# Gated attention outputs transposed on VectorE, with blocks exchanged through DRAM, in one transformer layer on Trainium2

## The chip, the cores and the metric

The kernel runs on one core of one Trainium2 chip. The metric is the device time of one execution in microseconds (us), as the median of several runs. A core has five engines that work side by side, each with its own queue of instructions: TensorE (PE in the profile; its weight loads are listed apart as PEld), VectorE (DVE), ScalarE (ACT), GpSimd (POOL) and SyncE (SP), which here only issues transfers. They read and write the on-chip memory SBUF; TensorE writes its results into PSUM, which is used as eight banks of 128 x 512 fp32. Transfers between SBUF and DRAM are done by 16 DMA engines.

## The reference

The layer takes x of shape 8 x 256 x 256 (2048 tokens of width 256), normalises it, and adds to it an attention part and a feed-forward part. Cut to what matters here:

```python
xn = layernorm(x)
q, k = rope(xn @ Wq.T), rope(xn @ Wk.T)          # 16 heads of 128
v, g = xn @ Wv.T, xn @ Wg.T
s = clip(xn @ Ws1.T @ Ws2.T + bs2, -32, 32)      # 16 heads of 64 states
z = cumlogsumexp(s, axis=time); es, enz = exp(s), exp(-z)
A  = tril(q @ k.T * scale)
qv = softmax(enz * (A @ es))
W2 = tril((qv * enz) @ es.T)
o  = W2 @ v                                      # per head: tokens x 128
o_g = o * rsqrt(mean(o * o) + EPS) * g_norm_weight * (g * sigmoid(g))
attn = o_g.reshape(B, T, 16 * 128) @ Wo.T
ffn  = (gelu(xn @ Wgate.T) * (xn @ Wup.T)) @ Wdown.T   # weights are 4-bit codes with scales
out  = x + attn + ffn
```

The change concerns the step between `o_g` and the product with `Wo`. The product contracts over the 128 values of a head, so `o_g`, which comes out with tokens on the partitions, has to be turned until the values of a head lie on the partitions.

## The kernel before, in words

All data is fp32. The 2048 tokens are worked on in four groups of 512 (`G`), and the 16 heads in eight pairs. One step of the main loop is one group and one pair: 32 steps (`N`), and the loop runs over `n` from -1 to 32, because the work of a pair is spread over three turns of the loop. In turn `n` the kernel makes the queries and keys (`rope`) of step `n + 1`, the values, gates, scores, logits and softmax of step `n`, and the turning of the softmax, the weights, the outputs and the closing product of step `n - 1` or `n - 2`. Between them stand pieces of the feed-forward part (`ffn`), which are spread over the whole run by a planned number for each turn.

The order is written out by hand. `POS` gives each piece a place between 0 and 1 within its turn (`START` overrides it in the first turns, `NORM_AT` places the norm of the next group), the list of pieces is sorted by that place, and the pieces are called in that order. A piece issues its TensorE work at once and hands what follows on the other engines to a generator (`chain`). After each piece `tick` moves every open chain on by one stage; `need` ticks until the named chains are done. `new` takes a buffer of a tag and first lets the users of its previous tenant finish. So the order in which each engine's instructions stand is settled when the program is built; on the chip the engines wait for one another through semaphores.

The pieces around the change are these.

- `outputs` (L656), once for each head of a pair, multiplies the weights with the values into the PSUM bank `po`, four blocks of 128 tokens by 128 values (L665). Its chain squares them on ScalarE (L674, with a sum for each token), adds on VectorE (L678), takes the power -1/2 on GpSimd (L679), and writes the gated output `og` with four VectorE instructions, one for each block (L683). `og` is laid out token block by token block, each of 128 contiguous values.
- `turn_back` (L690), once for each head, transposes the four blocks of `og` on TensorE into a bank (L696), and ScalarE copies that bank to `ogT` (L700). In `ogT` the 128 tokens of a block are contiguous in each partition.
- `close` (L705) runs in every second turn, for two pairs together, in two halves of 256 tokens. Each half is eight matmuls (L714): two token blocks times four heads, with a block of `ogT` as the weights and 256 columns of `w_o` moving. The result is added to `res` on VectorE (L277, by `add_to`), and a finished part of `res` goes out to DRAM (L270).

An fp32 matmul is two passes on TensorE, each with its own weight load, so that the 256 matmuls of `close` stand in the profile as 512; a transpose is one pass.

SyncE's queue carries all other transfers: the weights of a step (`load_w`, L161, two transfers a step), the packed feed-forward weights (L227 and L228), the rows of x (L152), and the output. A transfer at its head that waits for a buffer holds up those behind it.

Other lines that the prediction names: L205 transposes the normalised rows, whose columns it takes two apart; L298 and L318 are the feed-forward gate and up products; L338 the down product; L444 the queries and keys; L455 their first rotation product on VectorE; L496 values and gates; L514, L517 and L504 the scores and their mask; L562 the maximum of the softmax; L255 the last stage of decoding a feed-forward weight; L632 and L633 the masked weights `wt`.

Of the kernel before, what the change touches and what calls it, by code (L numbers as in the profile page):

```python
# [10 lines left out]
F32 = mybir.dt.float32  # L11
# [6 lines left out]
P = 128  # L18
# [4 lines left out]
G = 512  # L23
NG = NTOK // G
TC = G // P
# [6 lines left out]

POS = {'scores': (0.059, 0.112),
 'turn': (0,),
 'logits': (0.144,),
 'softmax': (0.232,),
 'cross': (0.179,),
 'weights': (0.179, 0.193),
 'low': (0.072,),
 'states': (0.223,),  # L40
 'outputs': (0.364, 0.394),
 'back': (0.647, 0.688),
 'close': (0.136, 0.286),
 'rope': (0.36, 0.45, 0.487, 0.63),
 'vg': (0.458, 0.566, 0.766, 0.838)}
START = {-1: {'states': (0.544,), 'rope': (0.14, 0.43, 0.53, 0.63)},
# [5 lines left out]
     'rope': (0.198, 0.24, 0.32, 0.45)}}  # L52
FEED = {-1: (0.452, 1.0)}
NORMS = {0: 1, 2: 2, 5: 3}
NORM_AT = (0.2, 0.293, 0.427, 0.58, 0.75, 0.938)
FIRST = [0.35, 1.41]
LAST = [2.16, 2.05]
DUE = [4, 6, 7, 7, 8, 8, 9, 10, 11, 12, 12, 13, 14, 15, 15, 16, 17, 18, 19, 19, 19, 22, 23, 23, 24]
# [3 lines left out]
def layer_kernel(ctx: ExitStack, tc: tile.TileContext, a: dict, out: bass.AP):  # L62
# [19 lines left out]
    ln = ctx.enter_context(tc.tile_pool(name="ln", bufs=1))  # L82
    ff = ctx.enter_context(tc.tile_pool(name="ff", bufs=2))
    de = ctx.enter_context(tc.tile_pool(name="de", bufs=1))
    aw = ctx.enter_context(tc.tile_pool(name="aw", bufs=1))
    p1 = ctx.enter_context(tc.tile_pool(name="p1", bufs=1))
    p2 = ctx.enter_context(tc.tile_pool(name="p2", bufs=2))
# [5 lines left out]
    def need(*gens):  # L93

        while any(c in chains for c in gens):
            tick()
# [7 lines left out]
    def new(pool, shape, tag, bufs=1, dtype=F32):  # L104

        users = held.setdefault(tag, [])
        if len(users) >= bufs:
            need(*users[-bufs])
        t = pool.tile(shape, dtype, tag=tag, name=tag, bufs=bufs)
        users.append([])  # L110
        at_tag[id(t)] = t, users[-1]
        return t
# [3 lines left out]
    def chain(gen, *tiles):  # L116

        chains.append(gen)
        for t in tiles:
            at_tag[id(t)][1].append(gen)  # L120
        return gen

    def bank():
        return new(ps_p, [P, 512], "ps", 8)
# [233 lines left out]
    sin_b = sin.unsqueeze(1).to_broadcast([P, 2, T])  # L358
    of = {n: {} for n in range(N)}
    rTs = {}  # L360

    def load_wo():
        nc.sync.dma_start(out=gw, in_=a["gw"])
# [292 lines left out]
    def outputs(n, j):  # L656

        to = of[n]
        wt, c = to["wt", j]
        need(c, *(to["sg", i] for i in (0, 2)))  # L660
        v, sg, eps = to["v"], to["sg"], to["eps"]
        pot = to["po"][j]
        po = pot.rearrange("p (i d) -> p i d", d=DK)
        for i in range(TC):
            nc.tensor.matmul(  # L665
                po[:, i, :], lhsT=wt[:, i, :], rhs=v[:, i, j * DK : (j + 1) * DK],
                start=False, stop=i == TC - 1,
            )
        ss = new(p2, [P, TC], "ss", 2)
        og = new(p2, [P, TC, DK], "og", 2)  # L670

        def work():
            for i in range(TC):
                nc.scalar.activation(  # L674
                    og[:, i, :], po[:, i, :], AF.Square, accum_out=ss[:, i : i + 1]
                )
            yield
            nc.vector.scalar_tensor_tensor(ss, ss, 1.0 / DK, eps[:, j::2], ALU.mult, ALU.add)  # L678
            nc.gpsimd.tensor_tensor(ss, ss, nhalf, ALU.pow)  # L679
            yield  # L680
            yield
            for i in range(TC):
                nc.vector.scalar_tensor_tensor(  # L683
                    og[:, i, :], po[:, i, :], ss[:, i : i + 1],
                    sg[:, i, j * DK : (j + 1) * DK], ALU.mult, ALU.mult,
                )

        to["og", j] = og, chain(work(), pot, ss, og, eps, sg)

    def turn_back(n, j):  # L690

        og, c = of[n]["og", j]
        need(c)
        ps = bank()
        for i in range(TC):
            nc.tensor.transpose(ps[:, i * P : (i + 1) * P], og[:, i, :], ident)  # L696
        ogT = new(p2, [P, G], "ogT", 4)

        def work():
            nc.scalar.copy(ogT, ps)  # L700
            yield

        of[n]["ogT", j] = ogT, chain(work(), ps, ogT)

    def close(n, i):  # L705

        g, hp = steps[n]
        ogT = [of[m]["ogT", j] for m in (n - 1, n) for j in range(2)]
        need(*(c for _, c in ogT))
        pst = bank()  # L710
        ps = pst.rearrange("p (i d) -> p i d", i=2)
        for k in range(2):
            for hh in range(4):
                nc.tensor.matmul(  # L714
                    ps[:, k, :], lhsT=ogT[hh][0][:, (i + k) * P : (i + k + 1) * P],
                    rhs=w_o[:, (hp // 2) * 4 + hh, :], start=hh == 0, stop=hh == 3,
                )
        chain(add_to(g * TC + i, ps), pst)
# [11 lines left out]
    for n in range(-1, N + 1):  # L730
# [43 lines left out]
        if n > 0:  # L774
            put("turn", 0, turn, n - 1)
            put("cross", 0, cross, n - 1)
            put("weights", 0, weights, n - 1)
            put("weights", 1, apply, n - 1)
            for k in range(2):
                put("outputs", k, outputs, n - 1, k)  # L780
                put("back", k, turn_back, n - 1, k)
            if n % 2 == 1 and n > 1:
                for k in range(2):
                    put("close", k, close, n - 2, 2 * k)
            if n == N:
                for k in range(2):
                    put_at(2.0, close, N - 1, 2 * k)
# [80 lines left out]
```

## Time and profile before

The three runs took 1257.07, 1257.10 and 1257.87 us, median 1257.1. The profile is of one further execution:

| | |
|---|---|
| profiled execution, as timed | 1258.18 us |
| its span, first to last instruction | 1256.2 us |
| mean granted TensorE clock | 0.997 |
| DMA, all 16 engines | 47.96 MB in 18431 packets, mean 38 GB/s |
| weights load `wts`, 64 of 512 KB | 3.7 us from issue to landing (median) |
| output store `out_dram`, 8 of 256 KB | 2.2 us from issue to landing (median) |

The span lies inside the timed execution; the 2 us between them are outside the instructions. "Busy" is the time in which an engine has at least one instruction in work. Matmuls overlap in the pipeline, so the mean length of one is longer than the distance between the starts of two. Where the profile names a wait, it names the instruction whose end came last before the start. L numbers are lines of the kernel before unless the text says otherwise.

### The profile page before, as it was taken

The page shows a single profiled execution, that of the slowest core. Times are in us where ns is not written, and L with a number is a line of the kernel's source. Part 1 is how long each engine was busy: PE and PEld are TensorE (multiplying, and loading weights), DVE is VectorE, ACT ScalarE, POOL GpSimd, SP SyncE. Part 2 cuts the span into 40 slices and gives each one's busy share as a digit, 9 for nine tenths or more (in the row PEclk, how much of TensorE's full clock was granted, in tenths as well). Part 3 has the DMA queues.
Part 4 walks back from the last instruction along what each step waited for, and adds up shares of the span by engine and source line. Part 5 has one row for each costly group of instructions (what it writes and reads, how often), then busy time and mean ns, then how long its engine had stood idle before and what let it go on. Part 6 is the DMA issues. An engine that isn't in the chain of part 4 may idle for free.

```text
span 1256.2 us, 18066 instructions
## 1 busy us (share of the span) xinstructions
PE 1236.6 (98%) x6704; PEld 889.1 (71%) x6704; DVE 798.8 (64%) x1592; ACT 541.9 (43%) x1709; POOL 441.3 (35%) x408
## 2 busy tenths in 40 slices
PE   6999999999999999999999999999999999999998
PEld 3576776777776777767677676776777766777776
DVE  4977655767665676564776656666655566566443
ACT  3344435444344544443543534445443355444232
POOL 3524334432244443233442423444232444322311
PEclk9999999999999999999999999999999999999999
DMA  5211111011111100111110111110011110101100
GB/s 158 84 49 51 51 34 51 19 33 34 51 35 34 51 18 18 34 35 51 50 35 1 34 34 51 34 34 25 10 34 34 35 34 28 41 17 34 34 17 17
DMA packets 18431, 47.96 MB, mean 38 GB/s; under 512 B 2020, under 2 KB 6500, under 8 KB 18344
## 3 DMA queue, kind: packets, MB, share of 16 engines
q1 hardware_dynamic: 17912, 46.55, 11.8%
q8 instruction: 53, 0.87, 0.3%
q10 hardware_dynamic: 432, 0.26, 0.1%
q14 instruction: 34, 0.28, 0.1%
HBM read 44.71 MB, written 2.10 MB: 37 GB/s over the span
## 4 chain that ended last, share of the span: by engine, by line
PE 92%; DVE 5%; DMA 1%; issue 1%; POOL 1%; ACT 0%; POOLq 0%; ACTq 0%; SPq 0%; DVEq 0%
PE ps L496 16%; PE ps L444 16%; PE ps L714 9%; PE ps L338 9%; PE ps L298 8%; PE ps L318 8%; PE ps L514 4%; PE ps L665 4%; PE ps L533 4%; PE ps L624 3%; PE ps L517 2%; PE ps L696 2%; PE ps L406 2%; PE ps L554 1%; DMA pk<-in_codes_dram 1%; PE ps L601 1%
## 5 line engine op out<-in xcount | busy, mean ns | idle before, releaser
L457 POOL TENSOR_TENSOR z<-z,sin 128x512 f32<-128x512 f32 x128 | 163.3, 1276 | 416.8 <-ACT z L454 416.2
L444 PE MATMUL ps<-xT,wts 128*128 128x512 f32 x512 | 243.5, 599 | 0.7 <-ACT xT L211 0.7
L496 PE MATMUL ps<-wts,xT 128*128 128x256 f32 x1024 | 236.6, 379 | 0.0
L496 PEld LDWEIGHTS ps<-wts,xT 128*128 128x128 f32 x1024 | 193.2, 190 | 57.4 <-issue 26.8
L444 PEld LDWEIGHTS ps<-xT,wts 128*128 128x128 f32 x512 | 95.2, 193 | 80.4 <-issue 72.6
L306 POOL TENSOR_SCALAR t<-t 128x512 f32<-128x512 f32 x64 | 40.4, 631 | 261.7 <-ACT t L304 259.6
L453 ACT COPY z<-ps 64x512 f32<-64x512 f32 x128 | 74.5, 582 | 129.7 <-PE ps L444 90.5
L298 PE MATMUL ps<-xT,w_gate 128*128 128x512 f32 x256 | 121.5, 597 | 4.3 <-DVE t L312 2.2
L318 PE MATMUL ps<-xT,w_up 128*128 128x512 f32 x256 | 120.5, 593 | 0.0
L433 DVE RECIPROCAL enz<-enz 128x128 f32<-128x128 f32 x128 | 117.0, 932 | 0.0
L338 PE MATMUL ps<-w_down,inter 128*128 128x256 f32 x512 | 115.9, 379 | 0.2 <-DVE inter L326 0.2
L714 PE MATMUL ps<-w_o,ogT 128*128 128x256 f32 x512 | 115.6, 379 | 0.0
L277 DVE TENSOR_TENSOR res<-ps,res 128x512 f32<-128x512 f32 x64 | 44.1, 689 | 112.3 <-PE ps L338 57.5
L714 PEld LDWEIGHTS ps<-w_o,ogT 128*128 128x128 f32 x512 | 95.7, 190 | 15.1 <-issue 2.6
L338 PEld LDWEIGHTS ps<-w_down,inter 128*128 128x128 f32 x512 | 96.0, 190 | 13.3 <-DVE inter L326 0.6
L458 POOL TENSOR_TENSOR q<-q,z 128x512 f32<-128x512 f32 x64 | 81.5, 1273 | 27.9 <-DVE q L455 23.8
L458 POOL TENSOR_TENSOR k<-k,z 128x512 f32<-128x512 f32 x64 | 81.3, 1270 | 19.3 <-DVE k L455 15.4
L455 DVE TENSOR_TENSOR k<-ps,cos 128x512 f32<-128x512 f32 x64 | 43.8, 684 | 63.2 <-ACT z L454 63.2
L683 DVE SCALAR_TENSOR_TENSOR og<-ps,ss,sgate 128x128 f32<-128x128 f32 x256 | 71.0, 341 | 19.4 <-POOL ss L679 18.6
L310 ACT ACTIVATE t<-t 128x512 f32<-128x512 f32 x64 | 40.3, 630 | 97.8 <-DVE t L308 97.8
L609 ACT COPY cross<-ps 128x256 f32<-128x256 f32 x32 | 11.9, 372 | 161.3 <-PE ps L601 160.8
L566 ACT ACTIVATE pr<-ps,mx 128x64 f32<-128x64 f32 x256 | 76.3, 323 | 12.1 <-DVE mx L563 12.1
(81 smaller groups left out, 2002.8 us busy)
## 6 DMA issues: line engine op xcount, KB each, us to landing
wts<-in_wqkvg_dram SPq DMA_DIRECT2D x64, 512.0 KB, 3.7
pk<-in_codes_dram SPq DMA_DIRECT2D x12, 256.0 KB, 4.6
sc<-in_scales_dram SPq DMA_DIRECT2D x12, 256.0 KB, 4.7
w_o<-in_wo_dram SPq DMA_DIRECT2D x4, 512.0 KB, 7.0
out_dram<-res SPq DMA_DIRECT2D x8, 256.0 KB, 2.2
res<-in_x_dram SPq DMA_DIRECT2D x3, 512.0 KB
res<-in_x_dram SPq DMA_DIRECT2D x2, 256.0 KB, 4.3
w_s<-in_ws_dram SPq DMA_DIRECT2D x4, 68.0 KB
```

The costliest lines, as they stand in the source:

```text
L298: nc.tensor.matmul(pg, lhsT=w_gate[:, c, ns], rhs=xT[:, c, gs], start=c == 0, stop=c == 1)
L318: nc.tensor.matmul(pu, lhsT=w_up[:, c, ns], rhs=xT[:, c, gs], start=c == 0, stop=c == 1)
L338: nc.tensor.matmul(ps[:, k, :], lhsT=inter[g, n][0][:, (i + k) * P : (i + k + 1) * P], rhs=w_dn[:, n, :], start=n == 2 * q, stop=n == 2 * ...
L433: nc.vector.reciprocal(r, r)
L444: nc.tensor.matmul(ps, lhsT=w[:, c, :], rhs=xT[:, c, g * G : (g + 1) * G], start=c == 0, stop=c == 1)
L453: nc.scalar.copy(z[0:64], pv[64:128])
L457: nc.gpsimd.tensor_tensor(z, z, sin_b, ALU.mult)
L458: nc.gpsimd.tensor_tensor(y, y, z, ALU.add)
L496: nc.tensor.matmul(ps[:, k, :], lhsT=xT[:, c, tt], rhs=w[:, which, c, :], start=c == 0, stop=c == 1,)
L566: nc.scalar.activation(pr[:, k, :], pv[:, k, :], AF.Exp, bias=mx[:, k : k + 1], scale=SCALE, accum_out=sm[:, k : k + 1],)
L683: nc.vector.scalar_tensor_tensor(og[:, i, :], po[:, i, :], ss[:, i : i + 1], sg[:, i, j * DK : (j + 1) * DK], ALU.mult, ALU.mult,)
L714: nc.tensor.matmul(ps[:, k, :], lhsT=ogT[hh][0][:, (i + k) * P : (i + k + 1) * P], rhs=w_o[:, (hp // 2) * 4 + hh, :], start=hh == 0, stop= ...
```

## The change

`turn_back` and its place in the order are gone. `outputs` now writes `og` with the four token blocks innermost: value by value, the four blocks side by side, so that each of the four gate instructions writes with a step of four elements (16 bytes). The squares, whose values nobody reads, still go to the same buffer in contiguous pieces. A second chain then waits for the first, transposes `og` in place on VectorE in blocks of 32 x 32 (`turn_blocks`, one instruction of 128 x 512 for each head), and exchanges the blocks: each band of 32 partitions is stored to a DRAM scratch `by_way` (four transfers of 64 KB in pieces of 512 bytes), and one transfer of 256 KB brings the scratch back as `ogT` (`exchange`). `ogT` too has the token blocks innermost, so that `close` reads its weights with a step of four elements. Some places in the order change as well.

```diff
 POS = {'scores': (0.059, 0.112),
  'turn': (0,),
- 'logits': (0.144,),
+ 'logits': (0.178,),
...
- 'low': (0.072,),
+ 'low': (0,),
...
- 'back': (0.647, 0.688),
- 'close': (0.136, 0.286),
+ 'close': (0.107, 0.365),
...
-NORM_AT = (0.2, 0.293, 0.427, 0.58, 0.75, 0.938)
+NORM_AT = (0.29, 0.293, 0.427, 0.58, 0.75, 0.938)
...
+    dram = ctx.enter_context(tc.tile_pool(name="dram", bufs=1, space=bass.MemoryType.DRAM))
...
+    def turn_blocks(t):
+        v = t.rearrange("p (c k) i -> p c i k", c=4)
+        nc.vector.transpose(v, v)
+
+    def exchange(to, t):
+        by_way = dram.tile([P, 4, 32 * TC], F32, tag="by_way", name="by_way", bufs=4)
+        for r in range(4):
+            nc.sync.dma_start(
+                out=by_way.rearrange("(c k) r x -> r k c x", c=4)[r],
+                in_=t[32 * r : 32 * (r + 1)].rearrange("p (c k) i -> p c (k i)", c=4),
+            )
+        yield
+        nc.sync.dma_start(
+            out=to.rearrange("p t i -> p (t i)"), in_=by_way.rearrange("p r x -> p (r x)")
+        )
...
         ss = new(p2, [P, TC], "ss", 2)
-        og = new(p2, [P, TC, DK], "og", 2)
+        og = new(p2, [P, DK, TC], "og", 2)
+        ogT = new(p2, [P, P, TC], "ogT", 4)
+        flat = og.rearrange("p d i -> p (d i)")
 
         def work():
             for i in range(TC):
                 nc.scalar.activation(
-                    og[:, i, :], po[:, i, :], AF.Square, accum_out=ss[:, i : i + 1]
+                    flat[:, i * DK : (i + 1) * DK], po[:, i, :], AF.Square,
+                    accum_out=ss[:, i : i + 1],
                 )
...
                 nc.vector.scalar_tensor_tensor(
-                    og[:, i, :], po[:, i, :], ss[:, i : i + 1],
+                    og[:, :, i], po[:, i, :], ss[:, i : i + 1],
                     sg[:, i, j * DK : (j + 1) * DK], ALU.mult, ALU.mult,
                 )
 
-        to["og", j] = og, chain(work(), pot, ss, og, eps, sg)
-
-    def turn_back(n, j):
-
-        og, c = of[n]["og", j]
-        need(c)
-        ps = bank()
-        for i in range(TC):
-            nc.tensor.transpose(ps[:, i * P : (i + 1) * P], og[:, i, :], ident)
-        ogT = new(p2, [P, G], "ogT", 4)
-
-        def work():
-            nc.scalar.copy(ogT, ps)
-            yield
-
-        of[n]["ogT", j] = ogT, chain(work(), ps, ogT)
+        def turned():
+            while first in chains:
+                yield
+            turn_blocks(og)
+            yield
+            yield from exchange(ogT, og)
+
+        first = chain(work(), pot, ss, og, eps, sg)
+        to["ogT", j] = ogT, chain(turned(), og, ogT)
...
                 nc.tensor.matmul(
-                    ps[:, k, :], lhsT=ogT[hh][0][:, (i + k) * P : (i + k + 1) * P],
+                    ps[:, k, :], lhsT=ogT[hh][0][:, :, i + k],
                     rhs=w_o[:, (hp // 2) * 4 + hh, :], start=hh == 0, stop=hh == 3,
                 )
...
             for k in range(2):
                 put("outputs", k, outputs, n - 1, k)
-                put("back", k, turn_back, n - 1, k)
```

## The prediction

> **What bounds the kernel now.** I read the page's busy shares first, then its slices, then the chain that ended last. Columns of the first line: busy us, share of the span, instructions.
>
> ```profile
> PE 1236.6 (98%) x6704; PEld 889.1 (71%) x6704; DVE 798.8 (64%) x1592; ACT 541.9 (43%) x1709; POOL 441.3 (35%) x408
> ...
> PE   6999999999999999999999999999999999999998
> ...
> PE 92%; DVE 5%; DMA 1%; issue 1%; POOL 1%; ACT 0%; POOLq 0%; ACTq 0%; SPq 0%; DVEq 0%
> ```
>
> TensorE is full in every slice but the first and the last, at a granted clock of 0.997, and 92% of the chain is its own work. So I asked for TensorE's waits alone (total us, times, longest):
>
> ```profile
> PE ps L205 <- DVE z L197: 7.9, 2, 7.3
> PE ps L298 <- DVE t L312: 2.2, 1, 2.2
> ```
>
> The whole list is eight rows and 16 us. Asked for 75 to 1235 us alone, it holds only the second row, one stall at 134 us; in 180 to 1235 TensorE is busy 1055.00 of 1055 us. A microsecond of its work removed there is a microsecond of the kernel, unless something else becomes late. Next come the groups by shape that the change touches (xcount | busy us, mean ns | idle before):
>
> ```profile
> L714 PEld LDWEIGHTS ps<-w_o,ogT 128*128 128x128 f32 x512 | 95.7, 190 | 15.1 <-issue 2.6 <-DVE at L504 0.5 <-ACT t L310 0.2
> ...
> L683 DVE SCALAR_TENSOR_TENSOR og<-ps,ss,sgate 128x128 f32<-128x128 f32 x256 | 71.0, 341 | 19.4 <-POOL ss L679 18.6
> ...
> L700 ACT COPY ogT<-ps 128x512 f32<-128x512 f32 x64 | 34.3, 585 | 1.5 <-PE ps L696 1.0
> L696 PE MATMUL ps<-ident,og 128*128 128x128 f32 x256 | 33.6, 273 | 0.0
> ```
>
> A matmul's 273 ns is its length through the pipe, not what it costs its successor. The cost is the distance of starts, from TensorE's timeline (start us, length us):
>
> ```profile
> 540.77 1.04 PE L696 MATMUL ps<-ident,og 128*128 128x128 f32 x8
> 541.64 1.88 PE L298 MATMUL ps<-xT,w_gate 128*128 128x512 f32 x4
> ```
>
> Eight transposes take 541.64 - 540.77 = 0.87 us, 0.109 us each. In the same way the 16 closing matmuls at L714 (521.78 to 525.23) are 0.216 us apart, and L665's 16 (528.66 to 530.45) 0.112.
>
> **What the Trainium skill says.** "TensorE: Matmul & The Clock Gate", Step-by-step: the next weights are loaded while the present matmul runs. The trace agrees: each load starts with the matmul before it. So a load costs nothing until it is longer than that matmul's 0.216 us. "SBUF — State Buffer", Door 1: the memory has 16-byte lines, and at least two hits in a line are needed for full rate. The changed close reads its weights four fp32 apart, one hit in a line. The only strided weights in this trace are the layer norm's, two fp32 apart, two hits in a line:
>
> ```profile
> 252.90 0.65 PEld L205 LDWEIGHTS ps<-ident,z 128*128 128x128 f32 x4
> 253.11 0.63 PE L205 MATMUL ps<-ident,z 128*128 128x128 f32 x4
> ...
> 253.58 0.60 PE L583 MATMUL ps<-ident,pr 128*128 128x128 f32 x4
> ```
>
> These four are 0.118 us apart ((253.58 - 253.11)/4) against 0.109, and their loads are 204 ns long against 141 ns for L696: here two hits are not quite free. "VectorE: DVE Perf Modes", The three transpose paths: VectorE transposes only within 32x32 blocks, and 311 ns for 128x128 bf16. No VectorE transpose stands in this trace.
>
> **The change part by part**, against the profiled execution: span 1256.2 us, 1258.2 us as timed, 1.1 us above the median of 1257.1.
>
> 1. Removed from TensorE: 32 steps x 2 heads x 4 transposes = 256 x 0.109 = 27.9 us. All stand after 94 us, where TensorE is full. The chain gives the same rows 2.1% of the span, 26.4 us. I take -27.9.
>
> 2. Removed from ScalarE: 64 copies x 0.585 = 37.4 us, and 64 uses of a PSUM bank. ScalarE is busy 43% and off the path: 0, a little slack for others.
>
> 3. Added to VectorE: 64 transposes of 128x512. Nearest rows by shape: the reduction L562 over 128x512 at 678 ns, and from above L255 into w_up, 1238 ns for 128x512. I take 0.68 us each, 43.5 us in all, and keep 0.6 to 1.24. The gate's four writes now go 16 bytes apart: 341 ns each if the step is free, some 474 if it doubles the 133 ns that 128 cycles at 0.96 GHz take (the page's clock, an estimate). VectorE rises from 799 to 843 us, at worst 912 of some 1230: 69 to 74%. In a step this is 1.4 us, at worst 3.5. Behind it in the queue stand k, q and res, then idle time:
>
> ```profile
> 571.01 1.13 DVE L683 SCALAR_TENSOR_TENSOR og<-ps,ss,sgate 128x128 f32<-128x128 f32 x4 [1.12 <-POOL ss L679]
> 572.05 0.68 DVE L455 TENSOR_TENSOR k<-ps,cos 128x512 f32<-128x512 f32 x1
> 572.65 0.68 DVE L455 TENSOR_TENSOR q<-ps,cos 128x512 f32<-128x512 f32 x1
> 574.29 0.69 DVE L277 TENSOR_TENSOR res<-ps,res 128x512 f32<-128x512 f32 x1 [0.96 <-PE ps L338]
> 577.28 0.69 DVE L455 TENSOR_TENSOR k<-ps,cos 128x512 f32<-128x512 f32 x1 [2.31 <-ACT z L454]
> ```
>
> The brackets hold 1.12, 0.96 and 2.31 us: the first transpose falls into the first, the second is made good by 577. Those waiting are PSUM banks and the scores, which TensorE reaches ten us later. I take 1.5 us over the whole run (0.05 a step); bounds 0 and 10 (0.3 a step).
>
> 4. The close's weights: 512 loads, now four apart. If the price goes by the element, as at step two, they stand 0.118 us apart and hide under 0.216: 0. At twice the unit spacing, 0.224, they cost 8 ns x 512 = 4 us; at 0.24, 12 us. I take 0 because step two cost only 9 ns more spacing; the upper end is a rival below.
>
> 5. Added transfers: per head four stores of 64 KB and one load of 256 KB, 64 x 5 = 320 issues, 33.6 MB. The DMA engines are about 12% busy. Rows for landing, from the page's list of issues: the 256 KB output store 2.2 us, the 512 KB weight load 3.7. SyncE's timeline at the start shows 0.33 to 0.46 us for most issues, so one exchange is 4 x 0.4 + 2.2 + 0.4 + 3.7 = 7.9 us, of which the issuing queue is held for 4.2. The order of the changed program shows, on SyncE, stores, load, stores, load, then the two weight loads of the step, so these go out up to some 8 us later; they are wanted after more than 20 us. The rows themselves are wanted at the next even step's close, some 17 us after 572 (the close at 590.24, about 1 us earlier now), against 0.7 + 7.9 plus the other head's 4.2 = 12.8. Hidden.
>
> 6. At the end that cover is thin. The last gate ends at 1235.9, and the close that needs it starts at 1245.20, its fourth matmul 1.3 us later; less the transposes gone from between (1.1 us), the rows are wanted at 1245.4. The first head's gate ends at 1232.9, its transpose at 1233.6, its load goes out at 1237.6. Then the second head's stores: +1.6 +2.2 +0.4 +3.7 = 1245.5. I take 0.5 us; bounds 0 and 2.5.
>
> 7. Moved: on TensorE each pair's second close stands after the first head's output matmuls, not before; the low-rank product, the logits and one norm shift by a few places. Nothing is issued twice; beside steps without a close, which run without waits today, the new order looks alike. 0; bounds -1 and +2.
>
> Sum: -27.9 + 1.5 + 0.5 + 0.5 (half of point 7's upper margin) = -25.4; 1258.2 - 25.4 = 1232.8 as profiled, 1231.7 beside the median. **Forecast 1232 us.**
>
> **The rivals.**
> A: the strided weights show partly, at 0.224 to 0.25 us: 512 x 8 to 34 ns, +4 to +17 us, 1236 to 1249. For it: one hit in a line is worse than two. Against: the step to two cost 9 ns.
> B: VectorE or the exchange becomes late in each step, because TensorE's step shrinks by 0.87 us while VectorE's queue grows by 1.4 to 3.5: +5 to +15 us, 1237 to 1247. Against: the idle brackets.
> C, slower: each new 16-byte line costs the load again. From step one to two the lines of a load double from 32 to 64 and its length grows by 63 ns; at 128 lines it would grow by 189. 0.112 + 0.189 = 0.301 us, 85 ns over the matmul, x 512 = 43.5 us: 1232 + 43.5 = 1275. It decides from 0.216 + 25.4/512 = 0.266 us a load.
> D: the program does what its words say; the order shows 64 transposes and 320 transfers and no L696. I give "it doesn't" nothing.
>
> **Numbers.** Forecast's own case 1228 to 1238: 0.60; A 0.12; B 0.10; C 0.15; around no change 0.03. A measurement here can tell 0.2%, 2.5 us. Faster 0.82 (the first three), same 0.03, slower 0.15 (C). The range takes in the case itself, A and B: 1228 to 1250.
>
> **What would show it.** Right: no L696, TensorE still at 98%, the closing matmuls 0.216 us apart, no row of waits on ogT above 2 us. Wrong at point 4: their spacing above 0.22. Wrong at 3: waits of TensorE on VectorE through the middle. Wrong at 6: an idle stretch before the last close.

## The result, and the profile after

The changed kernel took 1251.6 us as a median of seven runs (1250.65 to 1254.78), against 1257.1 before: a ratio of 0.9963, interval 0.9951 to 0.9974. It is faster, by 5.4 us, a fifth of what was forecast; 1251.6 lies just above the range's upper end. The profiled execution, the fastest of the seven, took 1250.65 us; its span is 1248.6, 7.5 us less than before (1256.17 and 1248.64 in the traces). So the pair of traces differs by 2 us more than the medians.

First the page of the changed kernel, its busy line and TensorE's slices:

```profile
PE 1222.9 (98%) x6448; PEld 889.8 (71%) x6448; DVE 866.9 (69%) x1656; ACT 508.5 (41%) x1645; POOL 442.4 (35%) x408
...
PE   6999899999999999999999999999999999999997
```

The 256 transposes are gone (6704 - 256 = 6448 instructions on PE), and PE is still the bound (98% busy, and 92% of the chain that ended last). Two signs stand against the forecast. PEld has lost 256 loads and yet is as busy as before, 889.8 us against 889.1: other loads grew. And two slices of PE have fallen: the fifth, some 125 to 156 us, from 9 to 8, and the last from 8 to 7. VectorE's 867 us lie between the two figures of the prediction (843 and 912).

The groups by shape that answer to those shown of before (xcount | busy us, mean ns | idle before):

```profile
L728 PEld LDWEIGHTS ps<-w_o,ogT 128*128 128x128 f32 x512 | 122.5, 328 | 2.3 <-issue 1.2 <-DVE inter L326 0.2
...
L704 DVE SCALAR_TENSOR_TENSOR og<-ps,ss,sgate 128x128 f32<-128x128 f32 x256 | 78.4, 434 | 19.8 <-POOL ss L700 19.8
L366 DVE STREAM_TRANSPOSE og<-og 128x512 f32<-128x512 f32 x64 | 73.7, 1152 | 2.2
```

A weight load of the close (L714 before, L728 now) is 328 ns long instead of 190, and the idle time before these loads has gone from 15.1 to 2.3 us: TensorE's loader hardly rests between them any more. A gate write takes 434 ns instead of 341. A VectorE transpose takes 1152 ns. What the loads cost is read from the starts, here in TensorE's timeline (start us, length us):

```profile
509.94 3.88 PE L728 MATMUL ps<-w_o,ogT 128*128 128x256 f32 x16
513.65 0.59 PE L532 MATMUL ps<-q,k 128*128 128x256 f32 x2
```

(513.65 - 509.94)/16 = 0.232 us from one closing matmul to the next, against 0.216. That is 0.26 us for the 16 of a group. In most groups it is more: where a product of 0.11 us stands ahead and not one of 0.43, the second closing matmul starts 0.336 us after the first (the group at 524.01), and the others are 0.233 apart as here. Such a group costs 0.38 us. In the trace 24 of the 30 groups within the run are of this kind. TensorE's waits (total us, times, longest):

```profile
PE ps L338 <- DVE inter L326: 4.4, 3, 2.1
```

This row stood at 0.2 us before; two of the three waits, 3.3 us, are at the end. No row names `ogT`. The scratch's transfers land in 1.8 us (a store of 64 KB) and 2.7 us (a load of 256 KB) by the page's list of issues.

To see where the time went, I took the start of the first weights product (L624 before, L642 now) of each step from both timelines and compared the distances. From here on a "turn" is the stretch that ends with such a start, counted from 0: turn 0 runs from the beginning to the first weights product, and the third turn is turn 2. Most turns are 0.49 us shorter: 0.87 us for eight transposes, less 0.38. The whole sum, in us:

| | forecast | read from the two traces |
|---|---|---|
| transposes off TensorE | -27.9 | -28.2 |
| weight loads of the close: 24 groups of 16 at 0.38, 6 at 0.26, the last 32 matmuls 0.56 | 0 | +11.2 |
| third turn (106 to 149 us): +3.05, where -0.87 (transposes) + 0.38 (loads) was due | within +1.5 | +3.5 |
| end, after the last step's weights product: +2.84, where -1.10 (transposes) + 0.56 (loads) was due | +0.5 | +3.4 |
| turns 5, 10, 14, 23 and 28, which lost their gain | +0.5 | +2.9 |
| sum | -25.4 | -7.2 |

The spans differ by -7.5; the other -0.3 is the start (-0.2), the last turn but one (-0.35) and three turns with +0.06 each.

The third turn's stretch in TensorE's timeline (in brackets the idle time before, and what ended it):

```profile
131.06 1.98 PE L298 MATMUL ps<-xT,w_gate 128*128 128x512 f32 x4 [0.61 <-DVE q L473]
...
134.03 0.85 PE L205 MATMUL ps<-ident,z 128*128 128x128 f32 x4 [0.99 <-DVE z L197]
...
136.24 0.66 PE L601 MATMUL ps<-ident,pr 128*128 128x128 f32 x4 [1.36 <-DVE t L312]
137.37 1.19 PE L532 MATMUL ps<-q,k 128*128 128x256 f32 x2 [0.47 <-issue]
138.35 0.63 PE L535 MATMUL ps<-q,k 128*128 128x128 f32 x2
```

Four stops, 3.4 us in seven microseconds, where the kernel before had one of 2.2. Then a pair of L532 needs 0.98 us to the next line (137.37 to 138.35); at 513.65 it needed 0.43. The clock says why. In the traces it is recorded as full or half, and it changes on a grid of 3.41 us (before, at 23.84, 27.25, 64.80 and 68.21 us). Stretches of that grid around the stops (stretch, length, busy us of PE, PEld, DVE, ACT, POOL, then the granted TensorE clock, DMA share, GB/s), first before and then after:

```profile
133.05:136.46 3.41, 1.89 (x5) 0.94 (x6) 2.06 (x4) 3.23 (x7) 1.31 (x2) 1.00 0.82 251
```

```profile
133.79:137.20 3.41, 1.51 (x8) 1.05 (x8) 2.21 (x5) 2.31 (x5) 1.74 (x2) 1.00 0.93 296
137.20:140.61 3.41, 3.25 (x10) 2.84 (x11) 1.97 (x4) 2.02 (x5) 3.25 (x4) 0.50 0.52 204
```

The kernel before keeps its full clock after the stretch with 1.89 busy us. In the changed kernel, after one with 1.51, the clock stands at half for the next 3.41 us. "TensorE: Matmul & The Clock Gate", Part 1, What's actually happening, in the Trainium skill says that the clock is either full or half, by how busy TensorE was in a free-running window of some 3.4 us. The traces agree: 0.50 or 1.00, on a grid of 3.41 us. So the third turn's +3.5 us is 1.3 us of longer stops (3.43 against 2.16), at most 1.7 of clock (half of 3.41), and a rest that was not followed. The clock also fits the spread: the seven runs lie at 1250.65 to 1251.25 us at a mean clock of 0.999, and at 1251.62 to 1254.78 at 0.991 to 0.996.

### The profile page after: what moved, and what is told of

The parts are those of the page before. It is cut to its first block, busy times and chain, and to the rows that moved or that the text cites. A ratio compares the mean times of both kernels' runs of the same rounds, so it can differ in the third digit from the quotient of the medians.

```text
span 1248.6 us, 18213 instructions
## 1 busy us (share of the span) xinstructions
PE 1222.9 (98%) x6448; PEld 889.8 (71%) x6448; DVE 866.9 (69%) x1656; ACT 508.5 (41%) x1645; POOL 442.4 (35%) x408
## 4 chain that ended last, share of the span: by engine, by line
PE 92%; DVE 4%; DMA 2%; issue 1%; ACT 1%; POOL 0%; ACTq 0%; SPq 0%; DVEq 0%; POOLq 0%
PE ps L514 17%; PE ps L462 17%; PE ps L728 10%; PE ps L338 9%; PE ps L318 8%; PE ps L298 8%; PE ps L683 4%; PE ps L532 4%; PE ps L551 4%; PE ps L642 3%; PE ps L535 2%; PE ps L424 2%; PE ps L572 1%; PE ps L619 1%; DMA pk<-in_codes_dram 1%; PE ps L668 1%
## 5 line engine op out<-in xcount | busy, mean ns | idle before, releaser
L462 PE MATMUL ps<-xT,wts 128*128 128x512 f32 x512 | 242.7, 597 | 0.7 <-ACT xT L211 0.7
L462 PEld LDWEIGHTS ps<-xT,wts 128*128 128x128 f32 x512 | 94.0, 191 | 79.3 <-issue 71.3
L728 PE MATMUL ps<-w_o,ogT 128*128 128x256 f32 x512 | 127.0, 402 | 0.0
L728 PEld LDWEIGHTS ps<-w_o,ogT 128*128 128x128 f32 x512 | 122.5, 328 | 2.3 <-issue 1.2
L338 PE MATMUL ps<-w_down,inter 128*128 128x256 f32 x512 | 116.4, 380 | 4.4 <-DVE inter L326 4.4
L338 PEld LDWEIGHTS ps<-w_down,inter 128*128 128x128 f32 x512 | 96.1, 190 | 18.9 <-DVE inter L326 5.6
L700 POOL TENSOR_TENSOR ss<-ss,nhalf 128x4 f32<-128x4 f32 x64 | 64.8, 1014 | 94.0 <-DVE ss L699 92.0
L704 DVE SCALAR_TENSOR_TENSOR og<-ps,ss,sgate 128x128 f32<-128x128 f32 x256 | 78.4, 434 | 19.8 <-POOL ss L700 19.8
L308 DVE TENSOR_TENSOR t<-ps,t 128x512 f32<-128x512 f32 x64 | 43.3, 677 | 55.3 <-POOL t L306 55.3
L584 ACT ACTIVATE pr<-ps,mx 128x64 f32<-128x64 f32 x256 | 76.2, 323 | 12.8 <-DVE mx L581 10.4
```

What stands on the lines that cost most here:

```text
L338: nc.tensor.matmul(ps[:, k, :], lhsT=inter[g, n][0][:, (i + k) * P : (i + k + 1) * P], rhs=w_dn[:, n, :], start=n == 2 * q, stop=n == 2 * ...
L462: nc.tensor.matmul(ps, lhsT=w[:, c, :], rhs=xT[:, c, g * G : (g + 1) * G], start=c == 0, stop=c == 1)
L584: nc.scalar.activation(pr[:, k, :], pv[:, k, :], AF.Exp, bias=mx[:, k : k + 1], scale=SCALE, accum_out=sm[:, k : k + 1],)
L704: nc.vector.scalar_tensor_tensor(og[:, :, i], po[:, i, :], ss[:, i : i + 1], sg[:, i, j * DK : (j + 1) * DK], ALU.mult, ALU.mult,)
L728: nc.tensor.matmul(ps[:, k, :], lhsT=ogT[hh][0][:, :, i + k], rhs=w_o[:, (hp // 2) * 4 + hh, :], start=hh == 0, stop=hh == 3,)
```

## The experiments

All against the kernel before, on one chip for each group, medians of the runs.

### Theory 1: the close's weights, four elements apart, cost 12 us

Rival: the 0.38 us a turn comes from VectorE or from PSUM banks that come free late. First, the changed kernel with a close that reads the same bytes in contiguous columns:

```diff
-                    ps[:, k, :], lhsT=ogT[hh][0][:, :, i + k],
+                    ps[:, k, :], lhsT=ogT[hh][0].rearrange("p t i -> p (t i)")[:, (i + k) * P : (i + k + 1) * P],
```

> The changed kernel, but the close reads its weights as contiguous columns of ogT (other numbers than the layer's, the same count of weights). Theory 1 (the step of four in the weight loads costs 0.38 us per closing group of 16 matmuls, 32 groups, 12 us in all): the closing matmuls return from 0.233 to 0.216 us apart, the loads from 328 to 190 ns, and the time falls from 1251.6 to about 1239.4 us. Rival (the loads are longer but hidden, the loss is elsewhere): spacing unchanged within 3 ns, 1250 to 1252 us.

Measured: 1241.2 us (1240.3 to 1244.0), ratio 0.987 (0.9854 to 0.9887), 10.4 us below the changed kernel. Most turns are 0.88 us shorter than before, not 0.49. Its groups:

```profile
L728 PEld LDWEIGHTS ps<-w_o,ogT 128*128 128x128 f32 x512 | 96.4, 192 | 14.9 <-issue 2.6 <-DVE inter L326 0.2
```

VectorE's transposes (1151 ns) and gate writes (432 ns) are as slow as in the changed kernel, and only the loads are short again: the 0.38 us is theirs. The third turn and the end are not cured. In the trace they are 4.35 and 5.3 us longer than before, and the clock stands at half for 6.83 us in each.

Second, the same price put into the kernel before, where everything else stays: ScalarE lays `ogT` out four elements apart and the close reads it so.

```diff
-        ogT = new(p2, [P, G], "ogT", 4)
+        ogT = new(p2, [P, P, TC], "ogT", 4)
...
-            nc.scalar.copy(ogT, ps)
+            nc.scalar.copy(ogT.rearrange("p t i -> p i t"), ps.rearrange("p (i t) -> p i t", i=TC))
...
-                    ps[:, k, :], lhsT=ogT[hh][0][:, (i + k) * P : (i + k + 1) * P],
+                    ps[:, k, :], lhsT=ogT[hh][0][:, :, i + k],
```

> The kernel before, with TensorE transposes, but ScalarE lays ogT out with the four token blocks innermost, so that the close reads its weights with a step of four. Theory 1: the same 12 us, 1257.1 to about 1269 us, closing matmuls 0.233 us apart. Rival: 1257 to 1260 us, whatever ScalarE's strided write costs being off the path.

Measured: 1268.6 us (1268.3 to 1268.7), ratio 1.009 (1.0075 to 1.0105): +11.4 us, and 0.38 or 0.26 us in nearly every turn.

```profile
L714 PEld LDWEIGHTS ps<-w_o,ogT 128*128 128x128 f32 x512 | 122.4, 328 | 2.6 <-issue 1.2 <-DVE at L504 0.2 <-ACT t L310 0.2
...
L700 ACT COPY ogT<-ps 128x512 f32<-128x512 f32 x64 | 65.3, 1127 | 1.1 <-PE ps L696 0.6
```

The loads have the 328 ns of the changed kernel, with no VectorE transpose in the program. ScalarE's copy doubles too, from 585 to 1127 ns, but ScalarE is off the path. Theory 1 holds from both sides.

### A step of two

If four apart is dear and two apart nearly free, as the layer norm's loads suggested, the layout can be changed to pairs of blocks, `og` as [P, 2, DK, 2], at the price of pieces of 256 bytes in the exchange:

```diff
-        v = t.rearrange("p (c k) i -> p c i k", c=4)
+        v = t.rearrange("p a (c k) i -> p (a c) i k", c=4)
...
-        by_way = dram.tile([P, 4, 32 * TC], F32, tag="by_way", name="by_way", bufs=4)
+        by_way = dram.tile([P, 2, 4, 64], F32, tag="by_way", name="by_way", bufs=4)
...
-        og = new(p2, [P, DK, TC], "og", 2)
-        ogT = new(p2, [P, P, TC], "ogT", 4)
+        og = new(p2, [P, 2, DK, 2], "og", 2)
+        ogT = new(p2, [P, 2, P, 2], "ogT", 4)
...
-                    og[:, :, i], po[:, i, :], ss[:, i : i + 1],
+                    og[:, i // 2, :, i % 2], po[:, i, :], ss[:, i : i + 1],
...
-                    ps[:, k, :], lhsT=ogT[hh][0][:, :, i + k],
+                    ps[:, k, :], lhsT=ogT[hh][0][:, (i + k) // 2, :, (i + k) % 2],
```

> The change with the token blocks laid in two pairs, two innermost: weights, gate writes and VectorE transposes go in steps of two elements, the stores in pieces of 256 bytes, twice as many. Theory 1: a load of step two stays under 0.216 us, so the close is back at 0.216 us apart and the time falls by 12 us to about 1239 us, a little lower if the gate's writes and the transposes become shorter too. Rival (the smaller pieces make the exchange late): spacing 0.216 but waits of the close on ogT, 1245 us or more.

Measured: 1239.2 us (1237.5 to 1241.0), ratio 0.9856 (0.9842 to 0.9871).

```profile
L728 PEld LDWEIGHTS ps<-w_o,ogT 128*128 128x128 f32 x512 | 99.3, 198 | 11.9 <-issue 2.4 <-DVE t L308 0.2 <-DVE at L522 0.2
L704 DVE SCALAR_TENSOR_TENSOR og<-ps,ss,sgate 128x128 f32<-128x128 f32 x256 | 71.1, 341 | 19.6 <-POOL ss L700 19.6
...
L366 DVE STREAM_TRANSPOSE og<-og 128x512 f32<-128x512 f32 x64 | 45.7, 714 | 2.2
```

One edit, three prices: a load 198 ns instead of 328 (and 0.216 us from start to start), a gate write 341 instead of 434, a transpose 714 instead of 1152. "SBUF — State Buffer", Door 1, asks for two hits in each 16-byte line for full rate: two fp32 of step two are two hits, one of step four is one. The loads (198 ns, and 190 when contiguous) and the gate writes (341 at both) agree with it; of the transpose no contiguous form was measured.

### Theory 2: VectorE's transposes hold TensorE up, in the third turn and at the end

The changed kernel with the exchange but without the transposes (this part is left out):

```diff
-            turn_blocks(og)
```

> The changed kernel without the 64 VectorE transposes (the blocks are exchanged but not turned). Theory 2 (the fuller VectorE queue makes TensorE wait in turn 2, before the last close and in five turns between, together some 9 us): TensorE's wait on inter L326 at the end and the long stretch at 130 to 137 us go, and the time falls to 1242 to 1244 us. Rival (these stalls come from the transfers or from the new places in the order): both stay, 1250 to 1252 us.

Measured: 1244.1 us (1243.9 to 1245.6), ratio 0.9898 (0.9883 to 0.9913), 7.5 us below the changed kernel. The third turn is 1.4 us shorter than before, not 3.05 longer, and keeps its clock:

```profile
133.16 0.66 PE L601 MATMUL ps<-ident,pr 128*128 128x128 f32 x4 [0.57 <-DVE t L312]
134.29 0.67 PE L532 MATMUL ps<-q,k 128*128 128x256 f32 x2 [0.47 <-issue]
```

The end is 0.6 us longer than before, not 2.8. The five turns without a gain stay. So the third turn's loss needs the transposes, and so does most of the end's. The other way round, the kernel before with one more VectorE transpose for each head, of the gated output that nobody reads any more:

```diff
             nc.scalar.copy(ogT, ps)
             yield
+            v = og.rearrange("p i d -> p (i d)").rearrange("p (c k i) -> p c i k", c=4, i=TC)
+            nc.vector.transpose(v, v)
...
-        of[n]["ogT", j] = ogT, chain(work(), ps, ogT)
+        of[n]["ogT", j] = ogT, chain(work(), ps, ogT, og)
```

> The kernel before with one more instruction a head and step: after ScalarE's copy of the TensorE transposes, VectorE transposes the dead gated output in place in the change's pattern (64 in all, about 1.15 us each as in the changed kernel, 74 us of VectorE); everything else, places too, as before. Theory 'VectorE load': as taking these 64 out of the changed kernel gave 7.5 us, most of it in the third turn and at the end, putting them into the kernel before costs in the same places, 1260 to 1265 us. Rival 'slack is enough': here the place in the order is another (later in the step, and nobody waits for the turned tile), so TensorE is held up by less than 1.5 us and the time is 1256.5 to 1259 us.

Measured: 1259.2 us (1258.4 to 1261.2), ratio 1.0017 (1.0011 to 1.0024), between the two expectations. Its transposes take 1138 ns. The third turn is 0.86 us shorter here, the twentieth is 1.1 longer, the end 1.2 longer, with the changed kernel's row, L338 on `inter`, among TensorE's waits (2.5 us, against 0.2 before).

So the same VectorE work, later in the order, costs 2 us, some of it at the end, and nothing in the third turn. In that turn it is not the amount of work alone that counts; what the transposes stand ahead of is the likely difference.

The end was tried in the kernel with a step of two, with one `tick` more before the last step's transposes:

```diff
             while first in chains:
                 yield
+            if n == N - 1:
+                yield
             turn_blocks(og)
```

> The kernel with a step of two, where only the last step's turned() waits one tick more before its two VectorE transposes, so that the MLP's inter goes ahead of them at the end. Theory: TensorE's waits on inter (2.8 us in 3 in e4_step2, all at the end) come from the transposes standing ahead of inter on VectorE; they fall below 1.2 us and the time to 1237 to 1238 us. Rival: inter is late for its own chain's sake, or the exchange, one tick (about 4 us) later, now ends behind the MLP's last products: the waits stay or turn into a wait of the last close on ogT, and the time is 1239 to 1243 us.

Measured: 1237.7 us (1234.9 to 1237.9), ratio 0.984 (0.9825 to 0.9854), against 0.9856 without it: by the medians 1.5 us, with intervals that overlap. The changed kernel at its end, VectorE, then TensorE:

```profile
1226.90 1.11 DVE L366 STREAM_TRANSPOSE og<-og 128x512 f32<-128x512 f32 x1
1227.90 0.65 DVE L326 SCALAR_TENSOR_TENSOR inter<-t,ps 128x512 f32<-128x512 f32 x1
```

```profile
1228.61 0.70 PE L338 MATMUL ps<-w_down,inter 128*128 128x256 f32 x2 [1.21 <-DVE inter L326]
1231.38 5.88 PE L338 MATMUL ps<-w_down,inter 128*128 128x256 f32 x26 [2.08 <-DVE inter L326]
```

The `inter` for which TensorE stops first stands behind the second head's transpose. The kernel with a step of two, which the edit starts from, and then the edit:

```profile
1217.41 0.70 PE L338 MATMUL ps<-w_down,inter 128*128 128x256 f32 x2 [0.23 <-DVE inter L326]
1220.19 7.44 PE L338 MATMUL ps<-w_down,inter 128*128 128x256 f32 x26 [2.08 <-DVE inter L326]
```

```profile
1215.09 0.68 DVE L326 SCALAR_TENSOR_TENSOR inter<-t,ps 128x512 f32<-128x512 f32 x1
1215.68 0.71 DVE L366 STREAM_TRANSPOSE og<-og 128x512 f32<-128x512 f32 x1
```

```profile
1219.19 5.88 PE L338 MATMUL ps<-w_down,inter 128*128 128x256 f32 x26 [1.73 <-DVE inter L326]
1224.91 7.07 PE L730 MATMUL ps<-w_o,ogT 128*128 128x256 f32 x32
```

With the shorter transpose the first wait is already down from 1.21 to 0.23 us, and with `inter` ahead it is gone. The second stays at 1.73 us, above the 1.2 that was expected. Its `inter` ends a chain from VectorE over ScalarE and back, and this chain starts behind the second head's transpose. The same wait in the kernel before, and without any VectorE transpose (e2_no_dve_turn):

```profile
1239.48 5.88 PE L338 MATMUL ps<-w_down,inter 128*128 128x256 f32 x26 [0.17 <-DVE inter L326]
```

```profile
1224.60 5.88 PE L338 MATMUL ps<-w_down,inter 128*128 128x256 f32 x26 [1.29 <-DVE inter L326]
```

The 1.1 us between them are about those of TensorE's own last transposes, which stood ahead of these products before. So at the end taking them off TensorE gained nothing: TensorE is ready earlier, and its data is not. Of the end's +3.4 us some 1.1 are of this kind; the other 2.3 go when VectorE's transposes are left out. What the tick gained in this pair of traces is more than the 0.6 us of shorter stops: without it the clock stood at half from 1219.97 to 1223.38, so that the 26 products took 7.3 us instead of 5.7. With the tick and without it the last close follows without a wait: the exchange is not late, even by a tick.

For the third turn three things were tried: the first norm place put back, GpSimd's later scalings of `w_o` moved one turn on, and a tick more before every transpose.

```diff
-NORM_AT = (0.29, 0.293, 0.427, 0.58, 0.75, 0.938)
+NORM_AT = (0.2, 0.293, 0.427, 0.58, 0.75, 0.938)
```

> The kernel with a step of two (e4_step2, 1239.2 us), with the first place of the norms (NORM_AT) put back from 0.29 to 0.2, so that a norm's statistics are no longer asked of VectorE right beside its second piece. Theory 'place': the stall in the third turn (2.95 us of TensorE before L601, on VectorE's t) comes from the norm's VectorE work being bunched there; with it spread again the stall falls below 1 us and the time to 1236 to 1237.5 us. Theory 'load': VectorE is full in that turn whatever the order (unpacking, norm, and now the transposes); the stall stays at 2 to 4 us, perhaps before another line, and the time at 1238 to 1241 us.

Measured: 1239.4 us (1238.3 to 1240.9), ratio 0.986 (0.9844 to 0.9877): as in the kernel with a step of two. A stall of 3.6 us stands before another line (L462, on `esT`). "Load" holds here, "place" falls. The other two start from e10_step2_places, described below:

```diff
             while first in chains:
                 yield
-            if n == N - 1:
-                yield
+            yield
             turn_blocks(og)
```

> e10_step2_places (1234.2 us), where turned() waits one tick more before its VectorE transpose in every step and not in the last alone, so that the rotary pieces q and k stand ahead of it on VectorE. Theory 'chain': the third turn's stalls (L298 on q 2.2 us and L601 on t 2.1 us in e10_step2_places) come down a chain: VectorE's transposes delay k, k delays GpSimd, GpSimd is then late with t; with k ahead of at least one transpose the two stalls shorten by 0.7 to 1.5 us together, some of the stretch at half speed behind them goes, and the time is 1232 to 1233.7 us. Rival 'the gate writes' (or another work of VectorE) delay k, not the transposes: both stalls stay, 1233.8 to 1236 us.

```diff
-            for h in range(0, H, 4):
-                put_at(0.3 + 0.04 * h, scale_wo, h)
+            put_at(0.3, scale_wo, 0)
+        if n == 3:
+            for h in range(4, H, 4):
+                put_at(0.3 + 0.04 * h, scale_wo, h)
```

> e10_step2_places (1234.2 us), where GpSimd scales the three later parts of w_o one turn later (n == 3, not 2; the first close needs only the first part). Theory 'chain by GpSimd': one of these pieces, 1.12 us, stands between k and the next rotary piece in GpSimd's queue while TensorE stalls behind that queue; without it the stalls in the third turn fall by about 1.1 us and the time to 1232 to 1233.5 us. Rival 'VectorE alone': GpSimd would wait for VectorE at that place anyway, 1233.7 to 1236 us.

> Both edits of e12_step2_yield and e13_step2_scale on e10_step2_places. If the third turn's stalls come down one chain through VectorE and GpSimd, the two gains add: 1230 to 1232.5 us, and the stalls on q and t are together below 2 us. If one of the two engines alone decides, the time is that of the better of the two runs within 0.5 us.

Measured: 1234.3 us (1233.6 to 1235.2), 1233.5 (1233.3 to 1234.2) and 1234.8 (1232.4 to 1235.5), ratios 0.9814, 0.9809 and 0.9814, against 0.982 (0.9805 to 0.9834): no difference that can be told, and none of the gains that were expected. In the trace of e10_step2_places the third turn kept its full clock, in those of these three it did not. The first of these settles nothing, since its edit did not reach the place: in the third turn VectorE still does both transposes ahead of `k`. The second shows that the stop only passes on: GpSimd starts on `t` 0.5 us sooner, reckoned from the turn's first weights product, and TensorE waits 2.8 us before L601 all the same, on ScalarE's `xT` instead of VectorE's `t`. In e10_step2_places and in both of these GpSimd first waits 2.16 us for VectorE's `k`, which stands behind both transposes. So in that turn several chains are late together, and which edit would free it stays open.

### Theory 3: the moved places cost, not the transposes

The five turns that lost their gain, half a microsecond each, kept that loss in all changed kernels so far. The kernel before with the moved places alone:

```diff
- 'logits': (0.144,),
+ 'logits': (0.178,),
...
- 'low': (0.072,),
+ 'low': (0,),
...
- 'close': (0.136, 0.286),
+ 'close': (0.107, 0.365),
...
-NORM_AT = (0.2, 0.293, 0.427, 0.58, 0.75, 0.938)
+NORM_AT = (0.29, 0.293, 0.427, 0.58, 0.75, 0.938)
```

> The kernel before, with only the moved places of the change (logits 0.178, low 0, close 0.107 and 0.365, first norm place 0.29); the transposes stay on TensorE. Theory 'places cost': the half microsecond that turns 5, 10, 14, 23 and 28 gained in the changed kernel (some 2.5 us in all) comes from the moved places, so the time is 1258.5 to 1260.5 us. Rival 'places cost nothing by themselves': 1256 to 1258 us, and the half microseconds come from VectorE or from the removed turn_back. A third: without the added VectorE work these places bring a gain of 1 us or more, below 1256 us.

Measured: 1260.1 us (1259.9 to 1261.8), ratio 1.0026 (1.0015 to 1.0036): +2.8 us. Turns 5, 10, 14, 23 and 28 are 0.54 to 0.60 us longer, and the others within 0.06, but for the start, which is 0.25 longer, and the third and the last but one, which are 0.3 shorter. Turn 10, before and then with the places moved:

```profile
443.03 1.52 PE L533 MATMUL ps<-at,es 128*64 128x256 f32 x16
444.38 0.61 PE L601 MATMUL ps<-v,es 128*64 128x128 f32 x8
444.92 1.16 PE L624 MATMUL ps<-prT,esT 64*128 64x128 f32 x16
```

```profile
443.56 1.90 PE L533 MATMUL ps<-at,es 128*64 128x256 f32 x14
...
446.05 1.16 PE L624 MATMUL ps<-prT,esT 64*128 64x128 f32 x16
```

The logits and the cross product need 2.49 us (443.56 to 446.05) instead of 1.89, and no wait is listed: this shows in starts alone. These products load only 64 columns of weights (128*64), and they come in pairs, one for each head. Before, in turn 10, they follow the close, and the two of the first pair start 0.007 us apart. With the close moved away they follow the last score product (L517), the first two start 0.267 us apart, and the heads stay out of step. Turns 14 and 28 show the same. In turns 5 and 23 it is the small products of L406 that need 1.04 us up to L554 instead of 0.66. Which of the places it is, in the kernel with a step of two and the free end (e6_step2_tail):

```diff
- 'logits': (0.178,),
+ 'logits': (0.144,),
```

> e6_step2_tail (1237.7 us) with the place of logits put back from 0.178 to 0.144, close as the change has it. Theory 'logits': the half microseconds of turns 5, 10, 14, 23 and 28 belong to the place of logits; they go, and the time is 1234.5 to 1236 us. Rival 'close': they belong to the places of close; they stay, and the time is 1237 to 1238.5 us.

Measured: 1237.1 us (1236.8 to 1238.3), ratio 0.9842 (0.9828 to 0.9857). The five turns are unchanged to 0.01 us. With `close` and `low` put back too:

```diff
- 'logits': (0.178,),
+ 'logits': (0.144,),
...
- 'low': (0,),
+ 'low': (0.072,),
...
- 'close': (0.107, 0.365),
+ 'close': (0.136, 0.286),
```

> e6_step2_tail (1237.7 us) with logits, close and low at the places of the kernel before. Theory 'places cost': e8_before_places lost 2.8 us by these places, so putting them back brings as much, 1234 to 1236 us. Rival: with VectorE's added work the old places cost elsewhere (the close stands nearer to the end of the exchange, or VectorE is late for at in the third turn), 1237 to 1240 us.

Measured: 1234.2 us (1232.5 to 1236.8), ratio 0.982 (0.9805 to 0.9834). The five turns are 0.54 to 0.59 us shorter, 2.85 in all: they belong to the places of `close` (`low` runs in three turns only), and in turns 10, 14 and 28, where the close stands before the logits again, the pairs start 0.007 us apart again. The third turn is 1.8 us shorter as well, for which no theory was made; in this trace it kept its full clock, in that of e6_step2_tail it did not. Why a product in front puts the pairs out of step in these five turns and hardly in others is open.

### The exchange

Last, the kernel with a step of two, where VectorE's transposes write straight into `ogT` and nothing goes through DRAM:

```diff
-            turn_blocks(og)
+            turn_blocks(ogT, og)
             yield
-            yield from exchange(ogT, og)
+            yield
```

> The kernel with a step of two without the exchange through DRAM: VectorE's transposes write straight into ogT, and the blocks are not brought to their places (this part of the computation is left out). Theory: the transfers are hidden everywhere, so the time stays within 1.5 us of e4_step2 (1238 to 1240.5 us). Rival: the transfers delay the weights, the packed codes or the last close; then it falls to 1232 to 1236 us.

Measured: 1237.8 us (1235.7 to 1239.1), ratio 0.9844 (0.9829 to 0.9858) against 0.9856 (0.9842 to 0.9871). From the third weights product to the last, all distances are equal to 0.01 us to those with the exchange. The medians are 1.4 us apart, with intervals that overlap; in the traces the third turn differs by 1.7. That is little to go by: e4_step2 and e6_step2_tail, whose programs are equal in that turn, differ there by 0.6. So 320 transfers and 33.6 MB cost nothing in 29 turns, and what they cost in the third, if anything, is not settled.

## Why the prediction failed

The direction was right and so was the size of the gain on TensorE; most of it was given back at four places. The step that failed most is the 0 of point 4: of the 18.2 us between the forecast's -25.4 and the traces' -7.2 it makes 11.2. The third turn has 2.0 of them more than point 3 allowed, the end 2.9, the moved places 2.4.

1. Point 1, -27.9 for the transposes: right, -28.2, though the last 1.1 us of it, at the end, turned into a wait.
2. Point 2, ScalarE's copies off the path: right. ScalarE's busy time fell by 33 us, and its copy could double (the second run of theory 1) without showing.
3. Point 4 failed, as a size. The step "I take 0 because step two cost only 9 ns more spacing" carried a price from two hits in a line to one hit. The runs show no price at two (198 ns, 0.216 us apart) and a large one at four: 328 ns, 0.233 us apart, in most groups one distance of 0.336, in all 11.2 us. This is close to the upper end that the point itself kept (12 us), and it is rival A, which had 0.12. Rival C, 0.301 us a load, fell: the loads are 328 ns long, but their starts are 0.233 apart, so that one load begins before the last has ended. That C's length for a load (141 + 189 = 330 ns) came out is luck: it took the 63 ns between two different groups for the price of step two, which within one group is 8 ns (190 to 198).
4. Point 3 failed, as a size and in its place. The transpose was put at 0.68 us with 1.24 kept as the upper end; it took 1.15. The gate's upper end (474 ns) came near to the 434 measured. The middle of the run bore it, as was argued from the idle brackets: no wait there names these instructions. But "1.5 us over the whole run" was spread evenly, while the cost lay in the one turn that had a stall already, row two of the waits before. There one stall became four stops and half a clock for 3.41 us: +3.5 us, and 4.5 against the run without the transposes. Its rival B was right only in this place.
5. Point 6, the end: the wait expected on `ogT` did not come. The transfers were quicker than taken (1.8 and 2.7 us for 2.2 and 3.7). What came were two waits on `inter`, behind the transposes in VectorE's queue and without the cover of TensorE's own: +3.4 us instead of 0.5, outside the point's bounds. The point followed the new rows through the transfers and did not ask who stands behind the new instruction, although that was asked for the middle.
6. Point 5, the exchange hidden: right.
7. Point 7, the moved places, 0 with a bound of +2: by themselves they cost 2.8 us. The step that failed is "beside steps without a close, which run without waits today, the new order looks alike": it looked for waits, and the cost was no wait but pairs of products out of step. In the sum the 0.5 is called half of the upper margin; half of +2 is 1, and 0.5 is the middle of the point's bounds. Nothing hangs on this, nor on a slip of 0.2 us in point 6 (1233.6 + 1.6 + 2.2 is 1237.4).

With the four put right as far as the runs could (a step of two, `inter` ahead of the transpose at the end, the old places), the kernel takes 1234.2 us, 2 us above the forecast and better than both kernels, at 0.982 (0.9805 to 0.9834). So nearly the whole gain of the forecast is there, but not with the layout that it was made for. What the sum lacked altogether is `inter`, the clock and the pairs; the prices of points 3 and 4 were taken near the lower ends of their own bounds.

## What to carry to other kernels

When a change alters a layout, price each reader and each writer of the tile at the new step: four fp32 apart made gate writes, weight loads and ScalarE's copy 27%, 73% and 93% longer here, and two apart cost nothing that showed in the time, so ask first whether half the interleave would do. Test a step that lengthens a hidden load against its cover: here 198 ns under 216 stayed hidden, and 328 did not, though it cost 17 ns a matmul and not the whole difference. With bounds on both sides the likeliest value should not be the cheap end when the only row seen lies on the cheap side of a threshold. Spread a new cost over the run by where slack is missing already (a stall in the waits, the end), not evenly, and at each such place ask who is queued behind the new instruction, and whether work that is taken away there was covering somebody's wait. When pieces change places, compare starts as well as waits.

## What the runs showed of the hardware

- Weight loads of 128x128 fp32: 190 ns with contiguous columns, 198 two apart, 328 four apart; under a 256-column matmul pass the starts are 0.216, 0.216 and 0.233 us apart, and with four apart 0.336 once in a group whose first load stands under a 0.11 us product.
- VectorE's transpose of 128x512 fp32 in place: 714 ns when its inner step is two elements, 1138 to 1152 when it is four. A gate write of 128x128: 341 ns contiguous or two apart, 434 four apart. ScalarE's copy of 128x512 from PSUM: 585 ns, and 1127 written four apart.
- TensorE's clock was full or half, and it changed on a grid of 3.41 us. In the third turns of all the traces, a stretch of this grid at full clock in which TensorE was busy for 0.48 of the time or less (1.51 us in the changed kernel) was followed by one at half clock, and a stretch with 0.51 or more by one at full clock. Elsewhere the border is not as sharp: in the kernel before, 2.29 busy us of 3.41 (61.39 to 64.80) were followed by half.
- Matmuls of 128 x 64 that use half the array ran in pairs, 0.007 us from start to start, when a longer product (0.2 us or more) stood ahead of them, from turn 1 on. Right behind a score product of 128 columns the first two started 0.06 to 0.27 us apart, and the stretch to the weights product took 1.95 to 2.49 us instead of 1.89.
